# Flamingo attention on one core: a row's largest score is carried from pass to pass on VectorE instead of being combined on GpSimd

## The chip, the cores and the metric

The kernel runs on one core of one Trainium2 chip. A core has five engines with queues of their own: TensorE (PE in the profile; its weight loads are shown as PEld), VectorE (DVE), ScalarE (ACT), GpSimd (POOL) and SyncE (SP), which here only issues DMA transfers. The engines run side by side and wait for one another through semaphores. The metric is the device time of one execution in microseconds, the median of several runs; lower is better. Before the change it is 1712.49 us (three runs, 1711.34 to 1713.07).

## The reference

The program is one block of gated cross-attention followed by a gated feed-forward part, over 2048 query rows (4 x 512) and 4096 context rows (4 x 1024), both 512 wide, 16 heads of width 32. The part that the change touches is the attention:

```python
q = (x @ Wq + bq).reshape(1, B * N, H, hd) * scale
k, v = split(cond @ Wkv + bkv)
q = _fq_sym(q, axis=-1)      # 8-bit: integers times one scale per row and head
k = _fq_sym(k, axis=-1)
v = _fq_sym(v, axis=2)
attn = jnp.einsum('bhqd,bhkd->bhqk', q, k)
attn = jax.nn.softmax(attn.astype(jnp.float32), axis=-1)
attn = _fq_unsigned(attn, axis=-1)   # 0..255 by the row's own maximum
out = jnp.einsum('bhqk,bhkd->bhqd', attn, v)
```

Every query row attends to all 4096 keys. The softmax needs the row's largest score, since the exponential is taken relative to it; here the same maximum also sets the 8-bit step of the attention weights, because the largest weight becomes 255. After the attention come the output projection, a gated residual, and a feed-forward part of width 2048 with quantised activations and ternary weights.

## The kernel before, in words

The program has three parts. Up to about 237 us it normalises and projects the rows, quantises queries and keys, and stores them to memory. From 237 us to about 1455 us it runs the attention. The rest is the feed-forward part.

The attention is a list of 256 **steps**: 16 heads times 16 tiles of 128 query rows. The order of the work is written out by hand: one loop goes over the steps, and inside a step over three chunks of the keys, `CHUNKS = ((0, 1536), (1536, 1536), (3072, 1024))`. All other work (the product of weights and values, the value projection of the next group of heads, later the first tiles of the feed-forward part) hangs in a plan keyed by step and chunk, and is issued at that place in the loop. Nothing is reordered afterwards, so each engine's instructions come in the order of this loop.

One step does the following.

- `scores(i, n)`, once for each chunk n. TensorE computes the integer scores of 128 rows against the chunk's keys (L726) into `ps_s`, a PSUM tile of which there are two. VectorE then makes one pass over the chunk (L735, `tensor_tensor_reduce`): it multiplies the scores by the keys' scales `skb`, writes the products to the score buffer `s`, and takes the row's maximum over the chunk into column n of `m3`, a tile of 128 rows and three columns. On the chip one such pass is two instructions: the pass itself (CUSTOM_DVE_ANT_0 in the profile) and a short one that reads the maximum out of the accumulator and writes it to `m3` (DVE_READ_ACCUMULATOR2_ANT; the profile calls the tile `m`).
- `exps(i)`, issued after the first chunk of the next step. GpSimd takes the maximum of the three columns of `m3` (L750, `m`), then forms `nb` = m times the negative scale of the query row plus ln 255 (L752). ScalarE takes the exponential of all 4096 scores with bias `nb` (L755), writes the result as one byte each into `r`, and sums the row.
- `turn_exps(i)`, two steps on: a transposing DMA on SyncE's queue turns `r` into `pT`.
- In later steps GpSimd widens the bytes of `pT` to 16 bits (L789, two instructions for each step, 1.89 us each), and TensorE multiplies them by the values (L805).

There are three score buffers: two tiles `s` and the memory called `third`. In the last 19 steps `third` is needed for the feed-forward part, and the two others take turns. A score buffer is free again when ScalarE has read it (L755), and that is what the first pass of a step waits for, besides its scores from TensorE.

A wait is carried out in one of two ways. An instruction can carry one wait itself. If it has more, the others are put into an instruction of their own ahead of it (EVENT_SEMAPHORE, shown on the queue DVEq for VectorE), which the engine's queue has to get past first. In the program before, the list of a first pass reads "TensorE, ScalarE", and that of most second and third passes "TensorE" alone.

The lines that the change and the prediction touch: L726 (scores), L735 (the three passes), L750 (maximum of three), L752 (`nb`), L755 (exponential), L789 (widening), and for comparison of costs L290 to L294 and L468 (quantising in the first part), L1053 (a residual), L1165 and L1172 (the layer norm of the last part).

Of the kernel before, what the change touches and what calls it, by code (L numbers as in the profile page):

```python
# [11 lines left out]
F32 = mybir.dt.float32  # L12
# [6 lines left out]
ALU = mybir.AluOpType  # L19
# [4 lines left out]
P = 128  # L24
# [9 lines left out]
def flamingo_kernel(  # L34
# [31 lines left out]
    nc = tc.nc  # L66
# [242 lines left out]
    with tc.tile_pool(name="pw", bufs=1) as pw, tc.tile_pool(  # L309
        name="pp", bufs=2  # L310
    ) as pp, tc.tile_pool(name="pl", bufs=5) as pl, tc.tile_pool(
        name="wr", bufs=2
# [237 lines left out]
        with tc.manual_schedule():  # L550
# [9 lines left out]
            n = len(order)  # L560
# [34 lines left out]
    CHUNKS = ((0, 1536), (1536, 1536), (3072, 1024))  # L595
    late = partial(tc.tile_pool, reuse_waits="tile")
    asb = ctx.enter_context(late(name="as", bufs=1))
    ar = ctx.enter_context(late(name="ar", bufs=3))
# [21 lines left out]
    def scores_buffer(i):  # L620
        return s_bufs[i % 3 if i < TWO else (i + 1) % 2]
# [90 lines left out]
    def scores(i, n):  # L712
        h, t = steps[i]
        kT, skb, qT = heads[h]
        if n == 0:
            live[i] = (
                scores_buffer(i),
                ar.tile([P, len(CHUNKS)], F32, name="m3"),
            )
        s, m3 = live[i]  # L720
        k0, w = CHUNKS[n]
        ps_s = asc.tile([P, CHUNKS[0][1]], F32, name="ps_s")
        for b in range(k0 // KB, (k0 + w) // KB):
            a, r = divmod(b, HPG)
            rows = slice(r * HD, (r + 1) * HD)
            nc.tensor.matmul(  # L726
                ps_s[:, b * KB - k0 : (b + 1) * KB - k0],
                qT[rows, 0, t * P : (t + 1) * P],
                kT[rows, 0, a * KB : (a + 1) * KB],
                start=True,  # L730
                stop=True,
                tile_position=(r * HD, 0),
            )

        nc.vector.tensor_tensor_reduce(  # L735
            s[:, k0 : k0 + w],
            ps_s[:, :w],
            skb[:, k0 : k0 + w],
            1.0,
            -3.0e38,  # L740
            ALU.mult,
            ALU.max,
            m3[:, n : n + 1],
        )

    def exps(i):
        h, t = steps[i]
        s, m3 = live.pop(i)
        m = ar.tile([P, 1], F32, name="m")
        nc.gpsimd.tensor_scalar(m, m3[:, 0:1], m3[:, 1:2], m3[:, 2:3], ALU.max, ALU.max)  # L750
        nb = ar.tile([P, 1], F32, name="nb")
        nc.gpsimd.tensor_scalar(nb, m, nsq[:, t, h : h + 1], LN255, ALU.mult, ALU.add)  # L752

        r = ar.tile([P, NK], U8, name="r")
        nc.scalar.activation(  # L755
            r.rearrange("p (n two) -> p two n", two=2),
            s.rearrange("p (two n) -> p two n", two=2),
            AF.Exp,
            bias=nb,
            scale=sq[:, t, h : h + 1],  # L760
            accum_out=rowsum[:, t, h : h + 1],
        )
        turning[i] = r
# [694 lines left out]
    with tc.manual_schedule():  # L1458
        nc.vector.memset(less, -128.0 * INT_STEP)
        nc.vector.memset(ones_h, 1.0)  # L1460
        for i in range(len(steps)):
            h, t = steps[i]
            for n in range(len(CHUNKS)):
                scores(i, n)

                if n == 0 and i in VALUES:
                    plan_group(*VALUES[i])
                if n == 0 and i:
                    exps(i - 1)
                for run in plan.pop((i, n), ()):  # L1470
                    run()
            if i > 1:
                turn_exps(i - 2)
            if h == 0:
                if t in LATE:
                    load_piece(1, LATE.index(t))
            elif h + 2 < H and t % 2 == 0:
                load_piece(h + 1, t // 2)
            if 0 <= i - PAIR < TG:
                for n in ((0, 4, 2), (1, 3), (5,), (6, 7))[i - PAIR]:  # L1480
                    load_piece(H - 1, n)
# [18 lines left out]
        act, pool = nc.scalar.copy, nc.gpsimd.tensor_copy  # L1500
        turn_exps(last - 2)
        exps(last - 1)
        turn_exps(last - 1)
        run(rest(last - 1, 3))
# [119 lines left out]
```

## Time and profile before

| | |
|---|---|
| time before, median of three runs | 1712.49 us (1711.34 to 1713.07) |
| the profiled execution: its time | 1714.34 us |
| the profiled execution: span from first to last instruction | 1712.5 us |
| VectorE busy | 1566.7 us, 91% of the span |
| TensorE busy | 1366.1 us, 80% |
| ScalarE busy | 1343.1 us, 78% |
| GpSimd busy | 1283.7 us, 75% |
| passes on VectorE, L735 | 768, of which 512 over 1536 keys and 256 over 1024 |
| accumulator reads, L735 | 768, 82 ns each on average |
| maximum of three on GpSimd, L750 | 256, 359 ns each on average |
| `nb` on GpSimd, L752 | 256, 265 ns each on average |
| exponentials, L755 | 256, 3.80 us each |
| granted TensorE clock, mean | 0.639 of full speed |

How to read it: busy time is the union of the times in which an engine executed something; waits and the issuing of transfers are not in it. A share over the whole span mixes the three parts of the program, so the attention is looked at by itself. In a timeline, each row gives start, duration, engine, line, operation and operands, and in brackets how long the engine had been idle before it and what ended that. A duration runs until the result is written, so a following instruction that depends on nothing may start a little before the previous one has ended.

### The profile page before, as it was taken

How to read it: one execution, taken by the hardware profiler on the slowest of the kernel's cores; microseconds unless marked ns; L12 is line 12 of the kernel's file. 1: busy time of each engine (PE TensorE's matmuls, PEld its weight loads, DVE VectorE, ACT ScalarE, POOL GpSimd, SP SyncE). 2: the span in 40 equal slices, each digit the busy share in tenths (PEclk: the TensorE clock that was granted, in tenths of full speed). 3: DMA queues.
4: the chain of work that ended last, by engine and by line, in shares of the span. 5: the costliest groups of instructions: out<-in, count | busy, mean ns of one | idle time of the engine just before them, and what ended most of it. 6: DMA issues, size and time to landing. Idle time of an engine off the chain costs nothing. (4 is left out here: it accounts for less than half of the span.)

```text
span 1712.5 us, 31561 instructions
## 1 busy us (share of the span) xinstructions
PE 1366.1 (80%) x12174; PEld 592.1 (35%) x12174; DVE 1566.7 (91%) x2205; ACT 1343.1 (78%) x988; POOL 1283.7 (75%) x1315
## 2 busy tenths in 40 slices
PE   8999968889966899886678998766666577789986
PEld 4444423333322333332233333222222233434432
DVE  5787889999999999999989999999999989578998
ACT  2443468888889798888978888898887877679987
POOL 0001226889999899999988999999999998656645
PEclk9999975555555555555555556555555555889998
DMA  6767969999999999999999999989999776613325
GB/s 208 274 248 249 300 189 225 194 211 212 181 200 189 212 189 207 208 197 202 173 208 185 227 181 215 202 171 198 165 198 179 151 140 130 169 50 87 89 53 117
DMA packets 736331, 315.92 MB, mean 184 GB/s; under 512 B 658034, under 2 KB 703670, under 8 KB 729782
## 3 DMA queue, kind: packets, MB, share of 16 engines
q1 hardware_dynamic: 727414, 309.19, 83.4%
q10 hardware_dynamic: 8736, 4.72, 1.1%
q8 instruction: 95, 1.56, 0.4%
q14 instruction: 54, 0.44, 0.1%
q0 software_dynamic: 32, 0.01, 0.0%
HBM read 110.15 MB, written 40.12 MB: 88 GB/s over the span
## 5 line engine op out<-in xcount | busy, mean ns | idle before, releaser
L789 POOL CAST rT<-pT 128x2048 int16<-128x2048 uint8 x506 | 944.1, 1892 | 28.9 <-DMA pT<-r 7.5
L735 DVE CUSTOM_DVE_ANT_0 s<-ps_s,skb 128x1536 f32<-128x1536 f32 x531 | 806.0, 1574 | 21.1 <-PE ps_s L726 13.0
L755 ACT ACTIVATE r<-s,nb,sq 128x4096 uint8<-128x4096 f32 x177 | 673.1, 3803 | 135.6 <-POOL nb L752 77.1
L726 PE MATMUL ps_s<-kT,qT 32*128 32x512 bf16 x2048 | 463.7, 593 | 245.7 <-DVE m L735 232.1
L735 DVE CUSTOM_DVE_ANT_0 third<-ps_s,skb 128x1536 f32<-128x1536 f32 (+1 forms) x237 | 362.6, 1574 | 5.5 <-PE ps_s L726 3.2
L755 ACT ACTIVATE r<-third,nb,sq 128x4096 uint8<-128x4096 f32 x79 | 300.3, 3802 | 46.7 <-POOL nb L752 34.0
L726 PEld LDWEIGHTS <-qT 32*128 32x128 bf16 x2048 | 95.4, 99 | 578.0 <-issue 571.1
L805 PE MATMUL acc<-rT,vq 128*32 128x128 f16 x8192 | 265.1, 307 | 33.3 <-ACT o L816 25.2
L805 PEld LDWEIGHTS <-vq 128*32 128x32 f16 x8192 | 196.8, 137 | 147.0 <-issue 105.1
L652 PE MATMUL vacc<-fx 128*128 128x256 f32 x384 | 231.4, 706 | 7.7 <-ACT fx L661 6.7
L750 POOL TENSOR_SCALAR m<-m 128x1 f32<-128x1 f32 x256 | 91.8, 359 | 67.8 <-DVE m L735 61.2
L472 POOL TENSOR_SCALAR nsq<-sq 128x16 f32<-128x16 f32 x16 | 3.2, 203 | 171.9 <-DVE sq L291 171.9
L652 PEld LDWEIGHTS vacc<-fx 128*128 128x128 f32 x384 | 94.9, 306 | 91.3 <-issue 79.2
L431 PE MATMUL kacc<-wk_sb,cT 128*128 128x512 f32 x256 | 117.7, 603 | 0.0
L752 POOL TENSOR_SCALAR nb<-m,nsq 128x1 f32<-128x1 f32 x256 | 67.8, 265 | 23.9
L1117 PE MATMUL ph<-fx,skb 128*128 128x512 bf16 x256 | 64.2, 396 | 0.1
L431 PEld LDWEIGHTS kacc<-wk_sb,cT 128*128 128x128 f32 x256 | 47.1, 194 | 47.6 <-issue 47.0
L735 DVE DVE_READ_ACCUMULATOR2_ANT m<- 128x1 f32 x768 | 62.7, 82 | 0.0
L431 PE MATMUL qacc<-wq_sb,xT 128*128 128x512 f32 x128 | 59.4, 608 | 0.1
L460 DVE TENSOR_TENSOR f<-kacc,bk_sb 128x512 f32<-128x512 f32 x32 | 22.0, 689 | 31.1 <-PE kacc L431 30.1
L300 ACT COPY cT<-tr 128x512 f32<-128x512 f32 x32 | 18.6, 580 | 34.8 <-PE tr L299 34.6
L360 POOL TENSOR_SCALAR wi<-wt 128x512 bf16<-128x512 int32 (+1 forms) x32 | 21.7, 704 | 31.5 <-ACT wt L356 19.3
(233 smaller groups left out, 1370.1 us busy)
## 6 DMA issues: line engine op xcount, KB each, us to landing
skb<-skd SPq DMA_DIRECT2D x32, 1024.0 KB
fx<-cTd SPq DMA_DIRECT2D x48, 512.0 KB
wt<-in_L_ffn_w_dram SPq DMA_DIRECT2D x16, 1024.0 KB
in<-in_ctx_dram SPq DMA_DIRECT2D x32, 256.0 KB
cTd<-cT SPq DMA_DIRECT2D x8, 1024.0 KB
q4d<-rows4q SPq DMA_DIRECT2D x16, 512.0 KB
vtd<-fx SPq DMA_DIRECT2D x24, 256.0 KB
fx<-vtd SPq DMA_DIRECT2D x24, 256.0 KB
```

What stands on the lines that cost most here:

```text
L360: nc.gpsimd.tensor_scalar(wi[:, a : a + w4], wt.bitcast(I32)[:, a : a + w4], 1.0, -1.0, ALU.min, ALU.max)
L431: nc.tensor.matmul(acc, tT[:, c, :], wk_sb[c] if kind == "k" else wq_sb[:, c, :], start=(c == 0), stop=(c == CC - 1),)
L460: nc.vector.tensor_tensor(f, acc, bk_sb, ALU.add)
L652: nc.tensor.matmul(state["acc"], wv_g[:, c, :], state["cT", j][:, c, :], start=(c == 0), stop=(c == CC - 1),)
L726: nc.tensor.matmul(ps_s[:, b * KB - k0 : (b + 1) * KB - k0], qT[rows, 0, t * P : (t + 1) * P], kT[rows, 0, a * KB : (a + 1) * KB], start=True,
L735: nc.vector.tensor_tensor_reduce(s[:, k0 : k0 + w], ps_s[:, :w], skb[:, k0 : k0 + w], 1.0, -3.0e38, ALU.mult, ALU.max, m3[:, n : n + 1],)
L750: nc.gpsimd.tensor_scalar(m, m3[:, 0:1], m3[:, 1:2], m3[:, 2:3], ALU.max, ALU.max)
L752: nc.gpsimd.tensor_scalar(nb, m, nsq[:, t, h : h + 1], LN255, ALU.mult, ALU.add)
L755: nc.scalar.activation(r.rearrange("p (n two) -> p two n", two=2), s.rearrange("p (two n) -> p two n", two=2), AF.Exp, bias=nb, scale=sq[: ...
L789: cast(spreads[k][:, 2 * u : 2 * u + 2, :, :] .bitcast(I16) .rearrange("p a (two b) q -> p a two (b q)", two=2), pTs[u][:, :, k * NW : (k ...
L805: nc.tensor.matmul(acc[c * HD : (c + 1) * HD, :], vq[:, kb, h % HPG * HD : (h % HPG + 1) * HD], rT[:, c, b, :], start=(k == 0 and b == 0), ...
L1117: nc.tensor.matmul(ph[:, n, :], xqT[:, c, tok], w1T[:, c, at : at + 512], start=(c == 0), stop=False,)
```

## The change

The maximum is no longer taken chunk by chunk and combined afterwards. The first pass starts from -3.0e38 as before; the second starts from the first pass's result, and the third from the second's, so that column 2 of `m3` holds the maximum over all three chunks. The initial value of the second and third pass is therefore no longer a constant but one value for each row, read from `m3`. GpSimd's maximum of three and its tile `m` are gone; `nb` reads column 2 of `m3` directly.

```diff
@@ def scores(i, n), the call at L735 @@
             ps_s[:, :w],
             skb[:, k0 : k0 + w],
             1.0,
-            -3.0e38,
+            m3[:, n - 1 : n] if n else -3.0e38,
             ALU.mult,
             ALU.max,
             m3[:, n : n + 1],
@@ def exps(i), L750 @@
         s, m3 = live.pop(i)
-        m = ar.tile([P, 1], F32, name="m")
-        nc.gpsimd.tensor_scalar(m, m3[:, 0:1], m3[:, 1:2], m3[:, 2:3], ALU.max, ALU.max)
+        m = m3[:, len(CHUNKS) - 1 :]
         nb = ar.tile([P, 1], F32, name="nb")
         nc.gpsimd.tensor_scalar(nb, m, nsq[:, t, h : h + 1], LN255, ALU.mult, ALU.add)
```

In the built program the order of the instructions on every engine is the same as before, except that the 256 instructions of L750 are missing on GpSimd. The list of waits of every second and third pass now reads "VectorE, TensorE".

## The prediction

> **What bounds the kernel now.** I read the page's busy line first, then the stages one by one, then VectorE's timeline inside the attention, and last the rows that price a wait and a per-row operand. The page's busy times, by engine:
>
> ```profile
> PE 1366.1 (80%) x12174; PEld 592.1 (35%) x12174; DVE 1566.7 (91%) x2205; ACT 1343.1 (78%) x988; POOL 1283.7 (75%) x1315
> ```
>
> Busy time by stage; the columns are the window, its length, and each engine's busy time and instruction count:
>
> ```profile
> 1100.00:1200.00 100.00, 61.75 (x880) 25.64 (x880) 100.00 (x139) 89.92 (x58) 94.76 (x89) 0.50 0.96 190
> 1200.00:1300.00 100.00, 61.96 (x880) 26.16 (x880) 100.00 (x135) 87.69 (x51) 96.53 (x90) 0.50 0.96 175
> 237.00:1353.00 1116.00, 852.85 (x9605) 360.47 (x9605) 1094.21 (x1478) 960.78 (x609) 1008.63 (x941) 0.51 0.99 195
> 1353.00:1455.00 102.00, 75.75 (x807) 32.92 (x807) 93.22 (x128) 76.96 (x48) 91.69 (x94) 0.50 0.73 141
> ```
>
> VectorE, third in the list, is busy 100.00 of 100 us; over the attention it idles 1116.0 - 1094.2 = 21.8 us and then 102.0 - 93.2 = 8.8 us, 30.6 us in all. Its timeline in there:
>
> ```profile
> 1283.03 1.75 DVE L735 CUSTOM_DVE_ANT_0 s<-ps_s,skb 128x1536 f32<-128x1536 f32 x1
> 1284.71 0.08 DVE L735 DVE_READ_ACCUMULATOR2_ANT m<- 128x1 f32 x1
> 1284.71 1.75 DVE L735 CUSTOM_DVE_ANT_0 s<-ps_s,skb 128x1536 f32<-128x1536 f32 x1
> 1286.39 0.08 DVE L735 DVE_READ_ACCUMULATOR2_ANT m<- 128x1 f32 x1
> 1286.39 1.22 DVE L735 CUSTOM_DVE_ANT_0 s<-ps_s,skb 128x1024 f32<-128x1024 f32 x1
> 1287.53 0.08 DVE L735 DVE_READ_ACCUMULATOR2_ANT m<- 128x1 f32 x1
> 1287.53 1.75 DVE L735 CUSTOM_DVE_ANT_0 s<-ps_s,skb 128x1536 f32<-128x1536 f32 x1
> ```
>
> A step takes 1287.53 - 1283.03 = 4.50 us, all of it VectorE's passes, each starting 0.07 us before the one ahead has ended, and at the very moment at which the accumulator read starts. TensorE has the next scores ready, so nothing but VectorE sets the pace. It has no room for a dependency between passes: the value that the second pass needs is written at 1284.71 + 0.08 = 1284.79, and the second pass now starts at 1284.71.
>
> **The change part by part.**
>
> *Removed: 256 instructions of L750 on GpSimd.* These are 256 x 359 ns = 91.8 us of busy time, and about 0.1 us between `m` and `nb` each time. GpSimd's own cycle in a step is m 0.35, nb 0.27, two casts 3.73 and the gaps, 4.5 us, as long as VectorE's; it falls to some 4.05. Off the path: VectorE alone fills the same 4.50 us. The path from the last pass to the exponential gets 0.45 us shorter, which helps only where VectorE waits for ScalarE; I count that below with the stalls.
>
> *Added: 512 waits of VectorE for itself.* The second and third pass of each step now wait until the accumulator read ahead of them is written. Behind the waiting pass stands everything else on VectorE's queue, in order; TensorE's next scores wait for the PSUM tile that this pass frees, and ScalarE for its scores. The price of such a wait is shown elsewhere. Chained VectorE instructions of the first part, and two of the last, then the extra waits as instructions on the queue:
>
> ```profile
> 152.35 0.69 DVE L290 TENSOR_REDUCE amax<-f 128x16 f32<-128x512 f32 x1
> 153.07 0.17 DVE L291 TENSOR_SCALAR sq<-amax 128x16 f32<-128x16 f32 x1
> 153.28 0.25 DVE L293 RECIPROCAL inv<-sq 128x16 f32<-128x16 f32 x1
> ```
>
> ```profile
> 1541.21 2.34 DVE L1165 SCALAR_TENSOR_TENSOR s<-s,nm,skb 128x2048 f32<-128x2048 f32 x1
> 1543.66 2.37 DVE L1172 SCALAR_TENSOR_TENSOR s<-s,rh,skb 128x2048 f32<-128x2048 f32 x1
> ```
>
> ```profile
> L1172 DVEq EVENT_SEMAPHORE  x7: 21/21/3107, 1515.6 to 1685.6; - x7
> ```
>
> In the first three rows each starts 0.03 to 0.04 us after the end of the one ahead (153.04 to 153.07, 153.24 to 153.28); in nanoseconds 34 to 37 wherever the wait for VectorE is the one the instruction carries itself. L1172 has two waits, "VectorE, GpSimd", and starts 104 ns after L1165 has ended (1543.55 to 1543.66): the record shows its EVENT_SEMAPHORE for VectorE's semaphore starting 38 ns after the end, 21 ns long, and the instruction 45 ns behind that. So the first wait in the list is the one that is split off, and the changed passes have "VectorE, TensorE": the dear form. I take 104 ns. A pass now starts 82 ns before the accumulator read ends and would start 104 ns after it: 186 ns x 512 = 95.2 us. The bounds are 34 + 82 = 116 ns (59.4 us), and a bit over 104 ns if the accumulator read tells its end later than other instructions do, for which there is no row.
>
> The Trainium skill, "VectorE: DVE Perf Modes", section "The DRAIN you can't avoid", says that a semaphore between VectorE instructions costs nothing extra (eight copies took 13.88 us with one after each or with one at the end). By that page the 95.2 us would be nothing and the estimate 1719 us; the rows above show 82 ns of overlap without a wait and a gap with one, so the rows decide.
>
> *Changed: the initial value is read for each row, 512 times.* The same operation with a constant and with a per-row operand, both with one input in PSUM:
>
> ```profile
> L468 DVE SCALAR_TENSOR_TENSOR f<-qacc,bq_sb 128x512 f32<-128x512 f32 x16 | 11.1, 692 | 14.8 <-PE qacc L431 14.8
> L1053 DVE SCALAR_TENSOR_TENSOR vq<-vacc,tg,vq 128x512 f32<-128x512 f32 x2 | 1.5, 748 | 0.0
> ```
>
> That is 748 - 692 = 56 ns; other rows spread from 27 ns (L1223 at its shortest, 719 ns) to 66 ns (L1172 at 2352 against L1178, a plain reduction of the same width, at 2286). L735 is a custom operation and may load the value beside other set-up, so the lower bound is 0. I take 56, the row nearest in form: 512 x 56 ns = 28.7 us, with 0 and 33.8 us as ends.
>
> *Given back: stalls.* VectorE's 30.6 us of idle time come from TensorE and ScalarE being late for a moment (value projection, transposes that land late at a change of heads, and two buffers instead of three in the last steps). A step that is 0.48 us longer gives these more time, and the shorter path to `nb` helps. I take three quarters, 23 us, as the many short ones (0.08 us) go wholly and the few long ones (2 to 4 us) in part; ends 0 and 30.6.
>
> *Costed at nothing:* the wait of `nb`, now "VectorE, ScalarE" instead of GpSimd's own, and an added wait of GpSimd for itself ahead of L789; they lie on GpSimd, which would be busy some 4.1 of 5.0 us. If that cover were gone they would cost what the split-off wait costs, 0.07 us a step. No DMA moves on any queue.
>
> **Sum.** A step becomes 4.50 + 2 x (0.186 + 0.056) = 4.98 us. Against the profiled execution: 1714.3 + 95.2 + 28.7 - 23 = 1815.2 us. That execution stands 1.9 us above the median of the runs, so the forecast for the median is 1813 us, 5.9% slower.
>
> **The rivals.** A difference under 0.2% (3.4 us) is about what a measurement of this kernel can't tell from none.
>
> - *The wait is cheap:* the pass carries the wait for VectorE itself, as L291 does. 59.4 + 28.7 - 23 = 65 us, 1778 us. The list's order and L1172 speak against it. 14%.
> - *The per-row value is free* in this operation: 95.2 - 23 = 72 us, 1785 us. For it: nothing but that L735 is another operation. 14%.
> - *Nothing is given back, or the accumulator read is dearer to wait for:* 1712.5 + 95.2 + 33.8 = 1841 us at the far end, 1836 with the middle price. For it: some stalls sit at fixed places of the plan, and transfers keep the DMA engines at a share of 0.99. Against: many stalls are shorter than what a step gains in time. 10%.
> - *Faster:* GpSimd, not VectorE, paces the steps; its cycle is also 4.5 us, and the chain of waits shows L789 as its largest line, 8%. With L750 gone and the pass not held up, only stalls could be won, at most 30.6 us: 1682 us. It decides only if wait and operand together cost under 30.6 / 512 = 0.06 us a pass; the 34 ns gap plus the lost overlap alone is 0.116. 3%, and 1% for no measurable change.
>
> My forecast itself, between 1798 and 1828 us as the stalls and the operand vary, has 58%. The range 1772 to 1838 us takes in the first two rivals and most of the third.
>
> **What the profile after would show.** Right: accumulator reads end, then some 0.10 us pass before the next pass starts; about 512 more split-off waits at L735 on VectorE's queue (294 before); passes of 1536 at 1.81 us for the second, 1.75 for the first; steps of about 4.98 us; GpSimd busy 92 us less; ScalarE's wait for `nb` (111.1 us before) nearly gone, since GpSimd is no longer late. Wrong: second passes still starting with the accumulator read, or 0.03 us behind it; second passes as short as first ones; or steps as before at the places where VectorE idled for others.

## The result: 6.2% slower, 1818 us where 1813 were forecast

The changed kernel takes 1818.34 us (median of four runs, 1816.56 to 1820.21) against 1711.91 us of the kernel before in the same session (1709.58 to 1713.07). The ratio is 1.062, with a 95% interval from 1.060 to 1.064. The profiled execution took 1817.03 us, its span is 1814.9 us, 102.4 us more than before, and its mean granted clock 0.630, where it was 0.639. The medians lie 106.4 us apart; the execution that was profiled before stands 2.4 us above its median, the one after 1.3 us below. Behind L749 the changed kernel's lines are one earlier (L752 is L751, L755 is L754).

The page's busy times of the kernel after, in the same order as before:

```profile
PE 1372.2 (76%) x12174; PEld 604.0 (33%) x12174; DVE 1629.8 (90%) x2205; ACT 1348.6 (74%) x988; POOL 1192.4 (66%) x1059
```

GpSimd lost 1283.7 - 1192.4 = 91.3 us, the 91.8 us of L750. VectorE gained 63.1 us of busy time. TensorE and ScalarE are busy about as long as before (6.1 and 5.5 us more). Busy time by stage, over stretches that were shown of before:

```profile
1100.00:1200.00 100.00, 70.39 (x825) 30.82 (x825) 94.72 (x125) 79.59 (x50) 77.75 (x59) 0.50 0.90 169
1200.00:1300.00 100.00, 54.32 (x765) 22.75 (x763) 94.35 (x122) 80.05 (x50) 78.21 (x60) 0.50 0.86 166
237.00:1353.00 1116.00, 812.37 (x8838) 351.93 (x8837) 1056.66 (x1358) 885.50 (x562) 844.43 (x644) 0.50 0.92 182
```

VectorE, the third engine, was busy 100.00 of 100 us in the first two stretches and is busy 94.7 and 94.4 now. Over the long stretch of the third row the other engines do less too than in the same 1116 us before (ScalarE, fourth, 885.5 against 960.8 us), and the share of the DMA engines, next to last, falls from 0.99 to 0.92: everything goes more slowly, and the engine that sets the pace has holes in its work. VectorE's timeline shows where the holes are:

```profile
1285.46 1.75 DVE L735 CUSTOM_DVE_ANT_0 s<-ps_s,skb 128x1536 f32<-128x1536 f32 x1
1287.14 0.08 DVE L735 DVE_READ_ACCUMULATOR2_ANT m<- 128x1 f32 x1
1287.37 1.82 DVE L735 CUSTOM_DVE_ANT_0 s<-ps_s,skb,m 128x1536 f32<-128x1536 f32 x1
1289.11 0.09 DVE L735 DVE_READ_ACCUMULATOR2_ANT m<- 128x1 f32 x1
1289.34 1.28 DVE L735 CUSTOM_DVE_ANT_0 s<-ps_s,skb,m 128x1024 f32<-128x1024 f32 x1
1290.55 0.08 DVE L735 DVE_READ_ACCUMULATOR2_ANT m<- 128x1 f32 x1
1290.55 1.75 DVE L735 CUSTOM_DVE_ANT_0 s<-ps_s,skb 128x1536 f32<-128x1536 f32 x1
```

The step is 1290.55 - 1285.46 = 5.09 us, where it was 4.50. The first pass of the next step, which needs nothing from the pass ahead, still starts at the moment of the accumulator read (1290.55 in the last two rows). The second and third pass start 0.15 us after the end of the read (1287.14 + 0.08 = 1287.22 to 1287.37). The passes with the per-row value are longer as well: 1.82 against 1.75 us. By form, with the mean duration in ns behind the busy time:

```profile
L735 DVE CUSTOM_DVE_ANT_0 s<-ps_s,skb,m 128x1536 f32<-128x1536 f32 x177 | 321.7, 1817 | 25.0 <-DVE m L735 0.5
L735 DVE CUSTOM_DVE_ANT_0 s<-ps_s,skb 128x1536 f32<-128x1536 f32 x177 | 310.4, 1754 | 2.0 <-ACT r L754 1.2 <-PE ps_s L726 0.8
L735 DVE CUSTOM_DVE_ANT_0 s<-ps_s,skb,m 128x1024 f32<-128x1024 f32 x177 | 227.2, 1284 | 25.2 <-PE ps_s L726 1.1
```

The last column is VectorE's idle time ahead of the group: 25 us each for second and third passes, 2 us for first ones (these are the 177 steps with a buffer `s`; in the 79 with `third` it is 11.4, 9.1 and 0.0 us). Before, 63 of the 72 passes that started late behind a read were first passes. The extra waits appear as instructions on VectorE's queue, at L735 763 of them where there were 294, most of them 21 ns long (minimum, median and maximum stand behind the colon; first before, then after):

```profile
L735 DVEq EVENT_SEMAPHORE  x294: 21/21/1700, 236.6 to 1447.2; - x147
L735 DVEq EVENT_SEMAPHORE  x763: 21/21/2631, 233.4 to 1555.2; - x191
```

**Where the time is.** From the first pass to the end of the last, the attention took 1217.3 us before and 1324.1 after: 106.8 us more. What lies ahead of it is 3.2 us shorter and what follows 1.2 us shorter, which makes the 102.4 us of the spans. The 106.8 us have three parts, in which the one mechanism of the forecast can be counted:

| part | working | us |
|---|---|---|
| a pass's wait for the read ahead of it | started 82 ns before its end, now 145 ns behind it: 227 ns x 480 | +109.0 |
| per-row value | 64 ns x 512 (1818 against 1754, 1284 against 1219) | +32.8 |
| given back | the rest | -35.0 |

There are 480 waits that cost something, not 512, because in 32 places another VectorE instruction lies between the two passes of a step. The timeline at one of them, where a reduction of the value projection (L671) is in between:

```profile
308.68 0.08 DVE L735 DVE_READ_ACCUMULATOR2_ANT m<- 128x1 f32 x1
308.68 0.68 DVE L671 TENSOR_REDUCE vmx<-fx 128x1 f32<-128x512 f32 x1
309.28 1.27 DVE L735 CUSTOM_DVE_ANT_0 third<-ps_s,skb,m 128x1024 f32<-128x1024 f32 x1
```

The pass has the same waits as all the others, yet it starts 0.08 us before L671 ends (308.68 + 0.68 = 309.36). What it waited for was done long ago, and the wait costs nothing. It is so in all 32 places: the pass starts 82 to 86 ns before the end of the instruction between.

### The profile page after: what moved, and what is told of

Read it like the earlier page. It is cut to its first block, busy times and chain, and to the rows that moved or that the text cites. A ratio compares the mean times of both kernels' runs of the same rounds, so it can differ in the third digit from the quotient of the medians.

```text
span 1814.9 us, 32015 instructions
## 1 busy us (share of the span) xinstructions
PE 1372.2 (76%) x12174; PEld 604.0 (33%) x12174; DVE 1629.8 (90%) x2205; ACT 1348.6 (74%) x988; POOL 1192.4 (66%) x1059
## 5 line engine op out<-in xcount | busy, mean ns | idle before, releaser
L754 ACT ACTIVATE r<-s,nb,sq 128x4096 uint8<-128x4096 f32 x177 | 674.0, 3808 | 193.4 <-POOL nb L751 193.4
L735 DVE CUSTOM_DVE_ANT_0 s<-ps_s,skb,m 128x1536 f32<-128x1536 f32 x354 | 548.9, 1550 | 50.2 <-PE ps_s L726 1.1
L754 ACT ACTIVATE r<-third,nb,sq 128x4096 uint8<-128x4096 f32 x79 | 300.9, 3809 | 89.1 <-POOL nb L751 86.7
L726 PEld LDWEIGHTS <-qT 32*128 32x128 bf16 x2048 | 108.5, 99 | 709.9 <-issue 695.9
L735 DVE CUSTOM_DVE_ANT_0 s<-ps_s,skb 128x1536 f32<-128x1536 f32 x177 | 310.4, 1754 | 2.0 <-ACT r L754 1.2
L735 DVE CUSTOM_DVE_ANT_0 third<-ps_s,skb,m 128x1536 f32<-128x1536 f32 (+1 forms) x158 | 244.9, 1550 | 20.5
L751 POOL TENSOR_SCALAR nb<-m,nsq 128x1 f32<-128x1 f32 x256 | 68.0, 266 | 296.7 <-DVE m L735 292.0
L735 DVE CUSTOM_DVE_ANT_0 third<-ps_s,skb 128x1536 f32<-128x1536 f32 x79 | 138.5, 1754 | 0.0
L735 DVE DVE_READ_ACCUMULATOR2_ANT m<- 128x1 f32 x768 | 64.5, 84 | 0.0
L431 PE MATMUL qacc<-wq_sb,xT 128*128 128x512 f32 x128 | 57.7, 593 | 0.1
L300 ACT COPY cT<-tr 128x512 f32<-128x512 f32 x32 | 18.6, 581 | 33.2 <-PE tr L299 33.0
```

The source lines that it names most:

```text
L300: nc.scalar.copy(tT, pt)
L431: nc.tensor.matmul(acc, tT[:, c, :], wk_sb[c] if kind == "k" else wq_sb[:, c, :], start=(c == 0), stop=(c == CC - 1),)
L726: nc.tensor.matmul(ps_s[:, b * KB - k0 : (b + 1) * KB - k0], qT[rows, 0, t * P : (t + 1) * P], kT[rows, 0, a * KB : (a + 1) * KB], start=True,
L735: nc.vector.tensor_tensor_reduce(s[:, k0 : k0 + w], ps_s[:, :w], skb[:, k0 : k0 + w], 1.0, m3[:, n - 1 : n] if n else -3.0e38, ALU.mult, A ...
L754: nc.scalar.activation(r.rearrange("p (n two) -> p two n", two=2), s.rearrange("p (two n) -> p two n", two=2), AF.Exp, bias=nb, scale=sq[: ...
```

## The experiments

Theory: each of the 512 dependent passes loses its overlap with the read ahead of it and pays a gap behind it, and pays for the per-row value besides; stalls give a part back. Rivals: the value alone is the price; the wait carries it all, or costs less than it seems; GpSimd sets the pace.

### The per-row value without the wait

The kernel before, with second and third passes that start from a tile written once at the beginning. Nothing depends on the pass ahead. Lines are two later than before.

```diff
+    low = keep.tile([P, 1], F32, name="low")
+    nc.vector.memset(low, -3.0e38)
...
-            -3.0e38,
+            low if n else -3.0e38,
```

> The kernel before, but the second and third pass take -3.0e38 from a column of memory written once at the start, so the operand is read for each row and no pass waits for another. If reading the operand costs 64 ns by itself (1818 against 1754 ns in the changed kernel), those passes last 1818 and 1284 ns and still start together with the accumulator read ahead of them; VectorE gets 512 x 0.064 = 33 us more work, of which the stalls give back half: 1712 + 33 - 17 = 1728 us, between 1718 and 1740. Rival: the 64 ns belong to a start after a wait, not to the operand: passes of 1752 and 1219 ns, 1712 us.

Measured: 1724.97 us, ratio 1.0083 (1.0060 to 1.0107) to the 1710.88 us of the kernel before on the same chip. VectorE's timeline in it:

```profile
1199.87 1.76 DVE L737 CUSTOM_DVE_ANT_0 s<-ps_s,skb 128x1536 f32<-128x1536 f32 x1
1201.55 0.09 DVE L737 DVE_READ_ACCUMULATOR2_ANT m<- 128x1 f32 x1
1201.55 1.82 DVE L737 CUSTOM_DVE_ANT_0 s<-ps_s,skb,low 128x1536 f32<-128x1536 f32 x1
1203.29 0.09 DVE L737 DVE_READ_ACCUMULATOR2_ANT m<- 128x1 f32 x1
1203.29 1.28 DVE L737 CUSTOM_DVE_ANT_0 s<-ps_s,skb,low 128x1024 f32<-128x1024 f32 x1
```

The passes start with the read (1201.55 and 1203.29 twice each), so no wait is left, and they are nearly as long as in the changed kernel: 1814 and 1279 ns at the median, against 1818 and 1284 there. With a constant they would be 1753 and 1219 ns, so some 61 of the 64 ns belong to reading the value, whatever it is and whoever wrote it; the last few come with the wait, as the next run shows. Of 512 x 61 ns = 31.2 us of added work 11.0 us remained in the attention; most of the rest took the place of stalls.

### The wait without the per-row value

The kernel before, with constants as initial values and GpSimd's maximum kept. The second input of the second and third pass is the part of `s` that the pass ahead has just written, where it was the key scales; the operation is an addition there, so that the attention's values differ.

```diff
-            skb[:, k0 : k0 + w],
+            s[:, CHUNKS[n - 1][0] : CHUNKS[n - 1][0] + w] if n else skb[:, k0 : k0 + w],
...
-            ALU.mult,
+            ALU.add if n else ALU.mult,
```

> The kernel before, with constants as initial values and GpSimd's maximum of three in place, but the second input of the second and third pass is what the pass ahead has written (added instead of multiplied), so each waits for it and no per-row operand is read. The attention's values are therefore others; the amount of work is the same. If the wait costs 227 ns by itself (82 of lost overlap and a gap of 145), 512 x 0.227 = 116 us, less some 40 of stalls: 1788 us, and the gap is 145 ns. Rival: 40 ns of the gap belong to fetching the operand, the gap is 104 ns as at the layer norm of the last part, and the time 1712 + 95 - 35 = 1772 us.

Measured: 1790.86 us, ratio 1.0470 (1.0445 to 1.0495). VectorE's timeline:

```profile
1099.75 1.75 DVE L735 CUSTOM_DVE_ANT_0 s<-ps_s,skb 128x1536 f32<-128x1536 f32 x1
1101.43 0.08 DVE L735 DVE_READ_ACCUMULATOR2_ANT m<- 128x1 f32 x1
1101.66 1.76 DVE L735 CUSTOM_DVE_ANT_0 s<-ps_s,s 128x1536 f32<-128x1536 f32 x1
1103.34 0.08 DVE L735 DVE_READ_ACCUMULATOR2_ANT m<- 128x1 f32 x1
1103.57 1.22 DVE L735 CUSTOM_DVE_ANT_0 s<-ps_s,s 128x1024 f32<-128x1024 f32 x1
```

The passes are about as short as before (1.76 and 1.22 us, 5 to 6 ns longer) and still start 0.15 us behind the read (1101.43 + 0.08 = 1101.51 to 1101.66; 144 ns in the records). So the gap belongs to the wait alone. The wait by itself costs 78.7 us of attention, about three quarters of the 106.8 us of the whole change, and the rival that the value carries the price falls.

### GpSimd's maximum gone, and nothing else

The kernel before without L750; `nb` is formed from column 2 of `m3`, which here is the maximum of the third chunk alone.

```diff
-        m = ar.tile([P, 1], F32, name="m")
-        nc.gpsimd.tensor_scalar(m, m3[:, 0:1], m3[:, 1:2], m3[:, 2:3], ALU.max, ALU.max)
+        m = m3[:, len(CHUNKS) - 1 :]
```

> The kernel before without GpSimd's maximum of three: the bias is formed from the third chunk's maximum alone, so it is not the row's largest score; the passes on VectorE are untouched. If VectorE paces the steps, a step without stalls stays at 4.50 us and only stalls can shrink: 1700 to 1711 us. Rival: GpSimd, whose work in a step is 4.5 us as well, paces them: steps fall under 4.50 us, and the time to 1685 us or less.

Measured: 1704.01 us, ratio 0.9961 (0.9946 to 0.9976). With 91 us less work on GpSimd, the steps still take 4.50 us, and the gain is 7 us. Busy time by engine in the 1116 us of the attention that were shown of before:

```profile
237.00:1353.00 1116.00, 854.60 (x9680) 362.16 (x9677) 1096.10 (x1484) 963.38 (x609) 929.21 (x708) 0.51 1.00 195
```

VectorE is busy 1096.1 us where it was 1094.2, and GpSimd 929.2 where it was 1008.6. GpSimd did not set the pace. The 7 us are all that the removed work was worth. This speaks against other forms of the change too: even one without any wait would pay for the per-row value, and on all second and third passes that value by itself made the attention 11.0 us longer.

### The wait in its cheap form

The changed kernel with a copy of one column of the scores ahead of each second and third pass. The copy takes over the wait for TensorE, and the pass is left with one wait, for VectorE. Lines are up to three later.

```diff
+        if n:
+            nc.vector.tensor_copy(seen[:, n : n + 1], ps_s[:, w - 1 : w])
```

> The changed kernel, with a copy of one score of the chunk to a spare column on VectorE ahead of each second and third pass. The copy takes the wait for TensorE, so the pass has only its wait for VectorE and carries it itself; the result is the same. If the gap is long because the wait is split off, it falls from 145 to 34 ns: 512 x 0.111 = 57 us less, 1761 us, or up to 10 more if the copy isn't wholly hidden behind the accumulator read. Rival: the gap belongs to starting this operation after a write it depends on; it stays near 145 ns and the time at 1818 us or a little above.

Measured: 1770.74 us, ratio 1.0349 (1.0328 to 1.0370): 512 added instructions on the busiest engine, and 47.6 us faster than the changed kernel. VectorE's timeline:

```profile
1100.46 1.75 DVE L738 CUSTOM_DVE_ANT_0 s<-ps_s,skb 128x1536 f32<-128x1536 f32 x1
1102.14 0.09 DVE L738 DVE_READ_ACCUMULATOR2_ANT m<- 128x1 f32 x1
1102.14 0.15 DVE L737 COPY seen<-ps_s 128x1 f32<-128x1 f32 x1
1102.26 1.82 DVE L738 CUSTOM_DVE_ANT_0 s<-ps_s,skb,m 128x1536 f32<-128x1536 f32 x1
1104.01 0.08 DVE L738 DVE_READ_ACCUMULATOR2_ANT m<- 128x1 f32 x1
```

```profile
L738 DVEq EVENT_SEMAPHORE  x268: 21/21/765, 236.2 to 1504.3; - x134
```

The split-off waits of the passes have fallen from 763 to 268, and in the records none of these is for VectorE's semaphore. The copy starts with the read and is over 0.06 us after it. The pass starts 1102.26 - 1102.23 = 0.03 us behind the read (35 to 36 ns in the records), not 0.15. So three quarters of the gap come from the wait being an instruction of its own, not from the dependency. The run changes one thing more, the copy that now stands between; but built-in operations that carry their wait start 34 to 37 ns behind the one ahead with nothing between. The step is 4.87 us.

### The carried value, with GpSimd's maximum kept

The kernel before with the first part of the diff alone; L750 takes the maximum of three columns of which the last is already the largest.

```diff
-            -3.0e38,
+            m3[:, n - 1 : n] if n else -3.0e38,
```

> The change's half on VectorE alone: the maximum is carried through the three passes, and GpSimd's maximum of three is still taken (it finds the same value). If the time is all VectorE's, steps take 5.09 us as in the changed kernel and the time is 1818 us within 5, since GpSimd's 4.5 us a step fit under 5.09. Rival: taking L750 away is worth something that the slower passes hide in the changed kernel: 1825 us or more.

Measured: 1821.01 us, ratio 1.0650 (1.0625 to 1.0674) to 1710.08 us. The step is 5.087 us as in the changed kernel, and the intervals of the two ratios overlap. So all of the loss comes from VectorE's part of the change.

### The value of the pass before the last

The kernel before, where the third pass alone starts from a computed value: the first pass's. GpSimd takes the maximum of the two columns that are left.

```diff
-            -3.0e38,
+            m3[:, 0:1] if n == 2 else -3.0e38,
...
-        nc.gpsimd.tensor_scalar(m, m3[:, 0:1], m3[:, 1:2], m3[:, 2:3], ALU.max, ALU.max)
+        nc.gpsimd.tensor_scalar(m, m3[:, 1:2], m3[:, 2:3], None, ALU.max)
```

> The kernel before, but the third pass starts from the first pass's maximum, two passes back, and GpSimd takes the maximum of the second and third. The third pass reads a fresh per-row value and needs no wait of its own for VectorE, since TensorE's scores for it already had to wait for the first pass. If the price is the wait for the pass right ahead, plus 64 ns for reading the value, the third pass starts with the accumulator read ahead of it and lasts 1284 ns; a step takes 4.56 us, 256 x 0.064 = 16 us more, half of it given back: 1719 us, between 1712 and 1727. Rival: a carried value holds the pass up wherever it comes from: a gap of 35 ns or more ahead of the third pass, a step of 4.68 us or more and 1740 us.

Measured: 1713.24 us, ratio 1.0016 (1.0001 to 1.0032). The end of a step's second pass and its third:

```profile
1201.68 0.08 DVE L735 DVE_READ_ACCUMULATOR2_ANT m<- 128x1 f32 x1
1201.68 1.28 DVE L735 CUSTOM_DVE_ANT_0 s<-ps_s,skb,m 128x1024 f32<-128x1024 f32 x1
1202.89 0.08 DVE L735 DVE_READ_ACCUMULATOR2_ANT m<- 128x1 f32 x1
```

A dependency over one pass in between costs nothing: the third pass starts with the read. It does have a wait of its own for VectorE, which the expectation had ruled out:

```profile
L735 DVEq EVENT_SEMAPHORE  x521: 21/21/1701, 235.9 to 1447.6; - x174
```

These are 227 more than before, and in the records 250 third passes have one for VectorE's semaphore. It is mostly over 0.14 us after the second pass has started, which runs 1.75 us, so even a split-off wait costs nothing when what it waits for was done long ago. What the third pass still pays is the per-row value, 256 x 60 ns = 15.4 us of VectorE's time, and of that only some 3 us arrive in the total (1713.24 against 1710.08 us).

### What the stalls gave back

The runs together show what became of VectorE's stalls. "Added" is the work and waiting that each edit put on VectorE's path, from the durations and gaps above; "attention" is the change of the time from the first pass to the last; "given back" is the difference. Each row is one profiled execution, and that of the kernel before stands 2 to 4 us above the medians of that kernel (1710.08 to 1711.91 us), so differences of that size say nothing. The last column is ScalarE's waiting for transposes of earlier exponentials, from the waits view of each run over the attention.

| run | added, us | attention, us | given back, us | ScalarE waits for transposes, us |
|---|---|---|---|---|
| kernel before | 0 | 0 | 0 | 53.8 (28 times) |
| maximum gone | 0 | -6.5 | 6.5 | 63.7 (36) |
| value over one pass | 256 x 0.060 = 15.4 | -1.1 | 16.5 | 44.3 (24) |
| per-row value alone | 512 x 0.061 = 31.2 | +11.0 | 20.2 | 37.3 (22) |
| wait in its cheap form | 480 x 0.118 + 32 x 0.066 + 32.8 = 91.5 | +57.7 | 33.8 | 13.0 (7) |
| wait alone | 480 x 0.226 + 512 x 0.006 = 111.6 | +78.7 | 32.9 | 6.6 (4) |
| carried value, maximum kept | 141.8 | +108.6 | 33.2 | 5.7 (3) |
| whole change | 141.8 | +106.8 | 35.0 | 2.4 (1) |

(The 32 x 0.066 us are the copy where another instruction stands ahead of it.) The first 15 us are given back nearly whole, and beyond some 90 us nothing more comes: the reserve is used up at 33 to 35 us. That is why the 78.7 us of the wait alone and the 11.0 us of the value alone do not add up to 106.8: each run draws on the same reserve. From the third row on the waits for transposes go down as the added work goes up; but with the maximum gone they rise, from 53.8 to 63.7 us, although 6.5 us came back. The two ends, of the kernel before and of the kernel after, in the views of ScalarE's waits over the attention (total, times, longest):

```profile
ACT r L755 <- POOL nb L752: 111.1, 148, 5.0
ACT r L755 <- DMA pT<-r: 53.8, 28, 4.3
```

```profile
ACT r L754 <- POOL nb L751: 280.1, 253, 3.4
ACT r L754 <- DMA pT<-r: 2.4, 1, 2.4
```

With longer steps hardly any transpose is late, and the DMA engines, at a share of 0.99 of the attention before, are at 0.92. That the missing waits for transposes are the stalls of VectorE that were given back is not shown: the two columns go together in six rows and not in the second, and no run changed the transposes alone.

## Why the prediction was right, by its own steps

The mechanism is the one forecast, and the total came 5 us beyond it. Its terms were off by more than the sum, in both directions, so that the total lies so near is partly luck: the wait came out 13.8 us dearer than forecast, the value 4.1 us, and against that 12.0 us more were given back:

| step of the prediction | predicted | measured | |
|---|---|---|---|
| the wait, for each pass | 82 ns of overlap + 104 ns | 82 + 145 ns | gap under-sized by 41 ns |
| passes that pay it | 512 | 480 | 32 have an instruction between |
| the wait in all | 95.2 us | 109.0 us | |
| per-row value | 56 ns, 28.7 us | 64 ns, 32.8 us | inside its bounds of 0 and 33.8 us |
| given back | 23 us | 35.0 us | beyond its upper end of 30.6 us; 2.7 us of it are no stalls |
| outside the attention | 0 | -4.4 us | unexplained |
| sum over the span | +100.9 us | +102.4 us | |
| VectorE's step | 4.98 us | 5.09 us | |

**The wait.** The price was read from L1172, the right form: a first wait of two, split off from the instruction. The record of the kernel after shows the same sequence, 39 ns to the split-off wait and 21 ns of it, but 85 ns to the pass where L1172 has 45. This custom operation begins later behind a split-off wait than the built-in ones do. That was there to be seen before: in the trace of before, more than 50 passes of L735 start 84 or 85 ns behind the end of a split-off wait. I had priced the wait from another operation's row where the operation itself had rows. The cheap form of the wait, a rival at 1778 us, was not what the kernel has, but the run that gave it that form came to 1770.74 us, so the rival's price was about right.

**The count.** I multiplied by all passes without looking for what lies between them. The 24 reductions of the value projection and eight other instructions do, in 32 places.

**The stalls.** I took VectorE's idle time, 30.6 us, as all that could come back. In the two traces the 35.0 us can be told apart. VectorE's idle time, without the 480 gaps, falls from 30.6 to 3.7 us: 26.9 us, so the guess of three quarters was too low, and little remained at fixed places of the plan. A late pass costs more than the idle time that it shows: it also loses the 82 ns by which it would have overlapped the read ahead. 72 passes of the kernel before start late behind a read; in the kernel after it is three, outside the 480 waits: 69 x 82 ns = 5.7 us. The other 69 VectorE instructions among the passes took 35.2 us and take 32.5, most of it in the casts of L686 (384 and 290 ns on average): 2.7 us that are no stall, and why is not known. Together these are 35.3 us.

**GpSimd.** Costed at nothing, and right: the run without L750 gained 7 us and no shorter step, and the run that kept it along with the carried value lost as much as the whole change.

**The signs.** Right were the gap behind the read, though 0.145 and not 0.10 us; more split-off waits, though 763 - 294 = 469 and not 512; second passes at 1.82 us; and GpSimd's 92 us. Wrong was that ScalarE's wait for `nb` would be nearly gone: it rose from 111.1 to 280.1 us. I had taken GpSimd's lateness for its cause. Now GpSimd itself waits for VectorE, and ScalarE, with 4.0 us of work in a step of 5.09 (the exponential's 3.80 and 0.19 for its sum), waits behind both; first before, then after:

```profile
POOL m L750 <- DVE m L735: 61.2, 71, 5.0
POOL nb L751 <- DVE m L735: 292.0, 246, 4.9
```

An engine that is off the path waits longer when the bound gets slower; the wait named the next link of the chain, not the cause.

**The skill's rule.** The Trainium skill, "VectorE: DVE Perf Modes", section "The DRAIN you can't avoid", says, from eight copies, that a semaphore between VectorE instructions costs nothing extra. By that rule the prediction's own terms give 1718 us, not the 1719 it states. The runs here disagree with the rule: the wait alone cost 78.7 us of attention, the unwaited passes overlapping the read by 82 ns and the waited ones standing 144 ns behind it. The same section says that one VectorE instruction in between removes the hazard of reading a small result too early. No run here tests that hazard. What the runs show is the cost: with one instruction between, the pass does not stand behind the read at all.

## What to carry to other kernels

On the engine that sets the pace, a result that the very next instruction needs costs the lost overlap and the gap of the wait, here 227 ns on passes of 1.2 to 1.8 us; the same result needed one instruction later costs nothing, so put other work between, or let the pass after the next use it. Where the dependency must stay, let the waiting instruction have that one wait only and give its other waits to something that is hidden. Work taken from an engine with a cycle as long as the bound's is worth little while the bound stands (7 of 91 us here), and before counting what waits will give back, add to the idle time the overlap that each late start loses.

## What the runs showed of the hardware

- A wait that is an instruction of its own, and ends last, costs this custom operation 40 ns more than built-in ones: 84 to 86 ns from the end of the split-off wait to L735, 44 to 46 ns to L1040, L1053 and L1172. Why is not settled. When what it waits for was done long ago it costs nothing (250 third passes in the run with the value of the pass before the last, which start with the read).
- A wait that an instruction carries itself costs this custom operation 35 to 36 ns, the same as the 34 to 37 ns of built-in operations. The form of the wait, not the dependency, made 145 ns out of it.
- A per-row initial value costs this custom operation some 60 ns on 1536 and on 1024 elements alike (61 and 60 with a constant column written long before; 64 and 65 with the carried value and its wait), so it is a cost for each instruction.
- A one-column copy between the accumulator read and the pass was wholly hidden in 480 places of 512: 0.15 us long, it starts with the read, and a pass behind it that waits for the read still starts at the read's end plus 35 ns. In the other 32 places, behind another instruction, it cost 66 ns.
